# The opening of a selective-scan layer: norms, weights and scratch banks in another order

## The chip, the core and the metric

The kernel runs on one core of a Trainium2 chip. The metric is the time of one execution in microseconds, from the device; lower is better. The engines are named as in the profile: PE (TensorE), PEld (its weight load), DVE (VectorE), ACT (ScalarE), POOL (GpSimd), SP (SyncE, which here only issues DMAs).

## What is computed

Four layers follow one another on an image tensor x of shape (2, 128, 64, 64), all in float32. Only layer 0 is touched here. Cut to what matters, it is:

```
x_norm = layernorm(x over the 128 channels, eps 1e-5) * w + b      # tokens: 4096 per image
for each of 4 token orders (rows, rows reversed, columns, columns reversed):
    xh, z = split(x_norm @ W_in.T)             # 256 inner channels each
    xh    = silu(causal_conv4(xh) + conv_b)
    dt, Bm, Cm = split(xh @ W_xp.T)            # 8, 16, 16 columns
    dt    = softplus(dt @ W_dt.T + b_dt)
    h_t   = exp(dt_t * A) * h_(t-1) + dt_t * Bm_t * xh_t     # 16 states per channel
    y     = (sum_n h_t[n] * Cm_t[n] + xh * Dp) * silu(z)
    out  += (y @ W_out.T) @ W_fuse[order].T
x = x + out + b_fuse
```

Layers 1 and 2 are attention over 4096 tokens, layer 3 is another small scan layer with a group norm.

## The kernel before

Channels lie on the 128 partitions and tokens along the free axis. Layer 0 is cut into 64 chunks of T = 512 tokens: 2 images x 2 orders x forward and reversed x 8. A chunk's 256 channels x 16 states are handled as 16 units of 128 partitions x 1024 elements. For each unit u: POOL forms `dbu` (`s_dbu`, L336), ACT the decay `da` (`s_da`, L349) into one of two PSUM pairs `das`, DVE runs the scan (`s_scan`, L380), DVE or POOL multiplies by C (`s_hc`, L392, L390), and PE sums over states into `y` (`s_y`, L403). Before a chunk's units can run, its front part has to: `px` and `x_` (the convolution folded into four products with `wk`, L238, L243), `xsilu` (L257), `pd` and `xd_` (L273, L278, the columns dt, B and C, whose rows go out to DRAM), `pt`, `abs_`, `e_exp`, `e_ln`, `dt_` (softplus, L293 to L312), `dtu_` (dt times x on POOL, L320), and `spread` and `states` (L328, L287), which store dt, dt times x and the rows of B and C to DRAM and load them back spread over the partitions as `dts`, `dus`, `bs` and `cs`.

The order of the work is written out by hand. Everything inside `tc.manual_schedule()` is issued in program order on each engine, and an engine that waits holds up all that stands behind it in its own order. The declarations above that block (memories set, weights loaded, weights folded) are placed by a planner. The loop over chunks interleaves the front part of the next chunks with the 16 units of the present one through the tables `A`, `V`, `M` and `G`; ahead of this loop stands the opening that is changed.

In the opening, SP loads x in eight pieces of 512 KB (L74). ACT issues the weights' loads: `vec`, `cst`, `m0`, the matrices `mt` (in a buffer of tag `h`), `w_dt` and `cwb` (in one of tag `hc`). DVE forms `wk` from `w_xT` and `cwb` (L125), and PE and DVE fold the output weights into `wof` (L130, L131). A norm of 512 tokens (`Norm0`) is a chain of eleven steps: mean by a product with `meanw` (L167), subtraction (L171), square (L175), variance by products of one column (L180), `keep`, Ln and Exp for the inverse root (L185 to L192), its spread into rows (L197), a product with `ones` (L201), a multiplication (L204) and the affine part into `xn` (L207). Three norms run first, then the front part of chunk 0, its da, dbu and z, the fourth norm, and px, x and silu of chunk 1.

PSUM has eight banks here: `misc` is one, `das` four, `pc` two, `y` one. In the opening every product but `pc` goes into the one bank `misc`:

```
for i in range(2):
    c.px(i)
    c.x_(i)
c.xsilu()
...
norm(3)
for i in range(2):
    c1.px(i)
    c1.x_(i)
c1.xsilu()
c1.pd()
```

Of the kernel before, what the change touches and what calls it, by code (L numbers as in the profile page):

```python
# [7 lines left out]
F32 = mybir.dt.float32  # L8
AF = mybir.ActivationFunctionType
ALU = mybir.AluOpType  # L10
# [3 lines left out]
P = 128  # L14
B, C, H, W = 2, 128, 64, 64
L = H * W
# [35 lines left out]
def _bc(ap, axis, shape):  # L52
    return ap.unsqueeze(axis).to_broadcast(shape)
# [3 lines left out]
def conv_seq_kernel(ctx: ExitStack, tc: tile.TileContext, a: dict, out: bass.AP):  # L57
# [6 lines left out]
    def gt(shape, name, pool=None, **kw):  # L64
        return (pool or gp).tile(shape, F32, tag=name, name=name, **kw)
# [3 lines left out]
    cst = gt([P, _NC], "cst")  # L69
    xin = a["x"].rearrange("b c h w -> c b (h w)")  # L70
    for b in range(B):
        for j in range(4):
            sl = slice(j * L // 4, (j + 1) * L // 4)
            nc.sync.dma_start(x[:, b, sl], xin[:, b, sl])  # L74
    nc.scalar.dma_start(vec, a["vec"])
    nc.scalar.dma_start(cst, a["cst"])
# [1 line left out]
    def v(name):  # L78
        return vec[:, _V[name] : _V[name] + 1]
# [14 lines left out]
    with ExitStack() as c0:  # L94
# [6 lines left out]
        def misc(shape=(P, T)):  # L101
            return ps.tile(list(shape), F32, tag="misc", name="misc")

        def wt(tag, bufs=None, shape=(P, 2, T)):
            return wk_.tile(list(shape), F32, tag=tag, name=tag, bufs=bufs)

        m0 = gt([P, 256 + 2 * ND], "m0", wp)
        nc.scalar.dma_start(m0, a["m0"][:, 0 : 256 + 2 * ND])
        w_zT = m0[:, 0:256]
        w_xpT = m0[:, 256:].rearrange("p (i m) -> p i m", i=2)  # L110

        mt = wt("h", NH, (P, 1024))
        nc.scalar.dma_start(mt, a["m0"][:, 256 + 2 * ND :])
        w_xT, w_out, w_fT = mt[:, 0:256], mt[:, 256:512], mt[:, 512:1024]

        meanw = gt([P, P], "meanw", wp)
        nc.vector.memset(meanw, 1.0 / C)
        w_dt = gt([ND, 256], "w_dt", wp)
        nc.scalar.dma_start(w_dt[64:ND, :], a["wdt"])
        cwb = wt("hc", shape=(P, 4, 256), bufs=NHC)  # L120
        nc.scalar.dma_start(cwb, a["cw0"].partition_broadcast(P))

        wk = gt([P, 4, 256], "wk", wp)
        for k in range(4):
            nc.vector.tensor_mul(wk[:, k, :], w_xT, cwb[:, k, :])  # L125

        wof = gt([P, 2, 4, P], "wof", wp)
        for i in range(2):
            pf = misc()
            mm(pf, lhsT=w_out[:, i * P : (i + 1) * P], rhs=w_fT, start=True, stop=True)  # L130
            nc.vector.tensor_copy(wof[:, i].rearrange("p d c -> p (d c)"), pf)  # L131

        sel = gt([48, NS, 32], "sel", wp)
        nc.vector.tensor_copy(sel[32:48], _bc(cst[32:48, _CI + 32 : _CI + 48], 2, [16, NS, 32]))
        sum4 = cst[:, _CR : _CR + 32]
        diag_d = gt([P, 2, P], "diag_d", wp)
        for i in range(2):
            nc.vector.tensor_scalar(diag_d[:, i, :], ident, v(f"dp{i}"), None, ALU.mult)
        zero = gt([P, 1], "zero", wp)
        nc.vector.memset(zero, 0.0)  # L140
        an = aneg[:, 0:32].rearrange("p (g b) -> p g b", g=4)
# [16 lines left out]
        class Norm0:  # L158
# [6 lines left out]
            def center(self):  # L165
                self.p = misc()
                mm(self.p, lhsT=meanw, rhs=x[:, self.b, self.sl], start=True, stop=True)  # L167
# [9 lines left out]
            def var(self):  # L177
                self.p = misc()
                for k in range(4):
                    mm(self.p[:, k : k + 1], lhsT=self.sq[:, k * P : (k + 1) * P],  # L180
                       rhs=meanw[:, 0:1], start=True, stop=True)
# [12 lines left out]
            def rows(self):  # L194
                self.sq = wt("sq", 1, (P, T))
                for k in range(4):
                    act(self.sq[:, k * P : (k + 1) * P], ident, AF.Copy, scale=self.r[:, k : k + 1])  # L197
# [8 lines left out]
            def affine(self):  # L206
                act(xn[:, self.dst], self.xc, AF.Identity, bias=v("ln_b"), scale=v("ln_w"))  # L207
# [8 lines left out]
        class Chunk:  # L216
# [14 lines left out]
                self.pt_, self.y, self.pc, self.xs = {}, {}, {}, {}  # L231


            def px(self, i):
                self.px_ = misc()
                for k in range(4):
                    off = self.t0 + (6 - k if self.rev else k)
                    mm(self.px_, lhsT=wk[:, k, i * P : (i + 1) * P], rhs=self.src[:, off : off + T],  # L238
                       start=(k == 0), stop=(k == 3))

            def x_(self, i):
                self.xs[i] = wt(f"xs{i}", shape=(P, T))
                act(self.xs[i], self.px_, AF.Identity, bias=v(f"cb{i}"))  # L243

            def pz(self, i):
                self.pz_ = misc()
                mm(self.pz_, lhsT=w_zT[:, i * P : (i + 1) * P],
                   rhs=self.src[:, self.t0 + 3 : self.t0 + 3 + T], start=True, stop=True)

# [16 lines left out]
                self.sz = wt("sz")  # L266
                nc.sync.dma_start(self.sz, gates[self.ci])

            def pd(self):

                self.p = misc()
                for i in range(2):
                    mm(self.p[:ND], lhsT=w_xpT[:, i, :], rhs=self.xs[i],  # L273
                       start=(i == 0), stop=(i == 1))
# [13 lines left out]
                                      self.rows[j, 4 * g + n, :].partition_broadcast(32))  # L288
                (self.cs if j else self.bs)[g] = t

            def pt(self, i):
                self.pt_[i] = misc()
                mm(self.pt_[i], lhsT=w_dt[64:ND, i * P : (i + 1) * P], rhs=self.xd[64:ND, :],  # L293
                   start=True, stop=True)

# [151 lines left out]
            pairs.setdefault(max(m + (3 if m in POOL_HC else 2) for m in (u, u + 1)), []).append(u)  # L447

        with tc.manual_schedule():
            def norm(j):  # L450
                n = Norm0(0, j)
                for f in (n.center, n.sub, n.square, n.var, n.keep, n.ln, n.exp, n.rows, n.scale,
                          n.mul, n.affine):
                    f()

            for j in range(3):
                norm(j)
            c, c1 = chunks[:2]
            for i in range(2):
                c.px(i)  # L460
                c.x_(i)
            c.xsilu()
            c.pd()
            c.xd_()
            for i in range(2):
                c.pt(i)
                c.abs_(i)
            c.e_exp()
            c.e_ln()
            for i in range(2):  # L470
                c.pt(i)
                c.dt_(i)
                c.dtu_(i)
            c.spread("dts", 0)
            c.states(0, 0)
            c.spread("dus", 0)
            for g in range(1, 4):
                c.states(0, g)
            for g in GROUPS_C:
                c.states(1, g)  # L480
            c.spread("dts", 1)
            c.spread("dus", 1)
            for i in range(2):
                c.pz(i)
                c.z_(i)
            c.s_pc(0)
            c.s_dbu(0)
            c.s_dbu(1)
            c.s_da(0)
            c.s_fix(0)  # L490
            norm(3)
            for i in range(2):
                c1.px(i)
                c1.x_(i)
            c1.xsilu()
            c1.pd()
            old = None
            for k, c in enumerate(chunks):
# [485 lines left out]
    with ExitStack() as c3:  # L984
# [65 lines left out]
        class Chunk3:  # L1050
# [17 lines left out]
            def xs_(self):  # L1068
                self.two(flat(lm), lambda i: x[:, self.b, self.sl])
                self.xs = wt("xs", bufs=3)  # L1070
                act(self.xs, self.p, AF.Silu, bias=v("cb3"))
# [418 lines left out]
```

## Time and profile before

| | |
|---|---|
| three timed runs | 6881.41 us median (6864.32 to 6891.15) |
| profiled execution, its own time | 6862.33 us |
| its span | 6860.5 us |
| DVE, POOL, PE, ACT busy over the span | 80%, 78%, 88%, 65% |
| first norm's first product / first px / xd of chunk 0 | 19.92 / 58.84 / 74.11 us |
| scan 0 / scan 1 of chunk 0 | 109.84 / 125.73 us |

Times of single instructions count from the span's start. A row of the time line gives start, duration, engine, line, operation, out<-in with sizes, and in brackets how long the engine had been idle and what released it. Shares over the whole span mix stages with different limits, so the stage that holds the change has to be looked at by itself.

### The profile page before, as it was taken

To read this page: it belongs to the slowest core of one execution; us is meant where nothing else is said; L and a number is where in the kernel's file an instruction comes from. 1 tells how busy PE (TensorE), PEld (TensorE's weight loads), DVE (VectorE), ACT (ScalarE), POOL (GpSimd) and SP (SyncE) were. 2 spreads that over 40 slices of the span, in tenths; PEclk is the share of its full clock that TensorE was granted. 3 is DMA by queue.
4 is the path that set the end of the run, shared out by engine and by line. 5 is a ranking of instruction groups with operands and counts; after the bars stand their busy time and mean duration, and the time that the engine had idled before them with its cause. 6 is when DMAs were issued, how large, how long until landed. Compare 5 with 4: busy or idle time off the path is not lost. (4 is left out here: it accounts for less than half of the span.)

```text
span 6860.5 us, 67328 instructions
## 1 busy us (share of the span) xinstructions
PE 6008.4 (88%) x20656; PEld 2820.0 (41%) x20656; DVE 5521.4 (80%) x4494; ACT 4472.9 (65%) x7688; POOL 5358.9 (78%) x2487
## 2 busy tenths in 40 slices
PE   6888888888888888888879999999999997988888
PEld 1222222222222222222227887787788884222222
DVE  3999999999999999999976665565566665877777
ACT  4887778877788777887756664455456554434343
POOL 3899999899999999999975665555556666777676
PEclk8777777778777777777769999999999998988898
DMA  3555565556565556656640000000000001222222
GB/s 108 139 150 148 148 155 141 138 149 150 142 159 153 150 146 156 155 143 152 155 117 6 3 5 1 1 1 1 1 1 13 1 1 54 69 76 75 87 69 75
DMA packets 352653, 616.52 MB, mean 90 GB/s; under 512 B 72473, under 2 KB 74786, under 8 KB 351906
## 3 DMA queue, kind: packets, MB, share of 16 engines
q1 hardware_dynamic: 351552, 610.44, 34.2%
q8 instruction: 162, 2.65, 0.2%
q14 instruction: 201, 1.65, 0.1%
q10 hardware_dynamic: 738, 1.78, 0.1%
HBM read 496.45 MB, written 115.47 MB: 89 GB/s over the span
## 5 line engine op out<-in xcount | busy, mean ns | idle before, releaser
L336 POOL TENSOR_TENSOR dbu<-dus,bs 128x1024 f32<-128x1024 f32 x1024 | 2402.8, 2372 | 173.0 <-DVE h L380 156.7
L380 DVE TENSOR_TENSOR_SCAN h<-da,hst,dbu 128x1024 f32<-128x1024 f32 x896 | 2090.9, 2341 | 77.3 <-ACT dbu L364 74.6
L349 ACT ACTIVATE da<-dts,aneg 128x512 f32<-128x512 f32 (+1 forms) x2048 | 1411.3, 689 | 438.1 <-DVE h L380 398.2
L832 POOL TENSOR_TENSOR sum<-sum,sc 128x1024 f32<-128x1024 f32 x384 | 906.3, 2360 | 495.6 <-ACT sc L827 491.9
L794 ACT COPY sc<-s 128x512 f32<-128x512 f32 x1024 | 597.9, 585 | 864.6 <-PE s L789 750.5
L789 PE MATMUL s<-q,k 128*128 128x256 f32 x4096 | 1053.3, 380 | 13.3 <-ACT q L775 8.4
L801 DVE TENSOR_TENSOR mx<-mx,s 128x512 f32<-128x512 f32 x896 | 609.4, 680 | 565.5 <-ACT sc L794 564.3
L844 PE MATMUL av<-sc,v 128*128 128x256 f32 x4096 | 1049.7, 379 | 2.3 <-ACT sc L827 2.3
L403 PE MATMUL y<-hc,cst 128*32 128x512 f32 x4096 | 811.6, 759 | 177.9 <-DVE hc L392 103.6
L392 DVE TENSOR_TENSOR hc<-h,pc 128x1024 f32<-128x1024 f32 x704 | 841.2, 1195 | 0.1
L789 PEld LDWEIGHTS s<-q,k 128*128 128x128 f32 x4096 | 777.8, 191 | 146.9 <-issue 36.6
L844 PEld LDWEIGHTS av<-sc,v 128*128 128x128 f32 x4096 | 769.1, 190 | 103.1 <-ACT sc L827 3.7
L390 POOL TENSOR_TENSOR hc<-h,cs 128x1024 f32<-128x1024 f32 x320 | 757.6, 2368 | 1.3 <-issue 1.3
L369 PE MATMUL pc<-xd,sel 16*128 16x512 f32 x1024 | 713.9, 789 | 3.4 <-DVE hc L392 2.6
L1159 POOL TENSOR_TENSOR A<-A,D 128x1024 f32<-128x1024 f32 x224 | 525.5, 2363 | 231.1 <-DVE D L1164 205.0
L824 DVE TENSOR_TENSOR sc<-sc,pm 128x1024 f32<-128x1024 f32 x512 | 620.4, 1212 | 0.9 <-PE pm L820 0.9
L827 ACT ACTIVATE sc<-sc 128x1024 f32<-128x1024 f32 x512 | 541.9, 1059 | 8.6 <-DVE sc L824 8.1
L293 PE MATMUL misc<-xd,w_dt 9*128 9x512 f32 x512 | 394.9, 860 | 157.3 <-ACT x L432 81.6
L1152 ACT ACTIVATE A<-dtr,aneg 128x1024 f32<-128x1024 f32 (+1 forms) x256 | 245.8, 1031 | 382.8 <-PE y L1184 365.3
L403 PEld LDWEIGHTS y<-hc,cst 128*32 128x32 f32 x4096 | 105.7, 117 | 743.2 <-issue 334.8
L1136 PE MATMUL q<-xs,lb 32*128 32x512 f32 x896 | 333.3, 714 | 71.8 <-DVE D L1146 64.8
L1170 DVE TENSOR_TENSOR A<-A,q 128x1024 f32<-128x1024 f32 (+1 forms) x256 | 276.7, 1081 | 141.6 <-PE q L1136 141.2
(210 smaller groups left out, 8079.0 us busy)
## 6 DMA issues: line engine op xcount, KB each, us to landing
dts<-ddt SPq DMA_DIRECT2D x512, 256.0 KB, 5.2
dus<-ddu SPq DMA_DIRECT2D x512, 256.0 KB, 4.8
bs<-rows SPq DMA_DIRECT2D x1024, 64.0 KB, 4.7
cs<-rows SPq DMA_DIRECT2D x1024, 64.0 KB, 3.2
ddt<-dt SPq DMA_DIRECT2D x128, 256.0 KB, 2.0
ddu<-dtu SPq DMA_DIRECT2D x128, 256.0 KB, 2.6
dtr<-ddt SPq DMA_DIRECT2D x448, 64.0 KB, 2.0
rx<-ddx SPq DMA_DIRECT2D x448, 64.0 KB, 1.9
```

The source lines that it names most:

```text
L336: nc.gpsimd.tensor_mul(t, self.dus[q], _bc(self.bs[g], 1, [P, 2, T]))
L349: act(t[:, i, sl], self.dts[q][:, i, sl], AF.Exp, scale=an[:, g, 2 * q + i : 2 * q + i + 1])
L369: mm(t, lhsT=sel[32:48, 4 * g : 4 * g + 4, :].rearrange("p n d -> p (n d)"), rhs=self.xd[32:48, :], start=True, stop=True)
L380: nc.vector.tensor_tensor_scan(ho, ai, bi, init, ALU.mult, ALU.add)
L390: nc.gpsimd.tensor_mul(t, self.h[u], _bc(self.cs[gq(u)[0]], 1, [P, 2, T]))
L392: nc.vector.tensor_mul(t, self.h[u], _bc(self.pc[u // 2], 1, [P, 2, T]))
L403: mm(self.y[q // 2][r : r + 32, :], lhsT=sum4, rhs=self.hc[u][:, i, :], start=False, stop=(u % 8 >= 6), skip_group_check=True)
L789: mm(p[:, o, :], lhsT=j.k[m // 8][:, m % 8 * P : m % 8 * P + P], rhs=self.q, start=True, stop=True)
L801: nc.vector.tensor_max(self.mx, self.s[0][:, 0:2, :] if u == 1 else self.mx, self.p[u])
L824: nc.vector.tensor_sub(s, s, _bc(self.pm[:, :], 1, [P, 4, NQ]))
L832: nc.gpsimd.tensor_add(self.sum, self.s[0] if w == 1 else self.sum, self.s[w])
L844: mm(self.av, lhsT=self.job.v[m // 8][:, m % 8, :], rhs=self.s[u // 2][:, m % 4, :], start=(m == 0), stop=(m == 31))
```

## The change

Only the opening of layer 0 changes, and the helpers that it calls:

- x of each image is loaded in pieces of 1, 1, 2 and 4 chunks in place of four of 2 chunks. The number of loads stays eight.
- ACT's loads are issued in the order `cwb`, `mt`, `m0`, `w_dt`. The folding into `wk`, `wof`, `sel` and `diag_d` moves into the ordered block.
- `px`, `pz`, `pd`, `pt` take a bank as an argument. The opening uses the four banks of `das` (`ba`) and those of `y` and `pc` (`bb`) as scratch.
- The first four norms are written out with their own buffers. The inverse root is Sqrt on ACT and a reciprocal on DVE in place of Ln and Exp. Norm 0 is completed ahead of chunk 0, norm 1 in step with it, norms 2 and 3 in pieces further on.
- `xs_` applies silu straight from the bank of px, in place of an Identity pass and a silu pass.
- On SP the sixteen loads of B precede the store and the spreads of dt. z is copied by DVE. `wof` is formed just ahead of the first scan.

The diff, cut to its core:

```diff
-        for j in range(4):
-            sl = slice(j * L // 4, (j + 1) * L // 4)
+        for lo, hi in ((0, 1), (1, 2), (2, 4), (4, 8)):
+            sl = slice(lo * T, hi * T)
             nc.sync.dma_start(x[:, b, sl], xin[:, b, sl])
...
+        nc.scalar.dma_start(cwb, a["cw0"].partition_broadcast(P))
+        nc.scalar.dma_start(mt, a["m0"][:, 256 + 2 * ND :])
         nc.scalar.dma_start(m0, a["m0"][:, 0 : 256 + 2 * ND])
+        nc.scalar.dma_start(w_dt[64:ND, :], a["wdt"])
...
-            def px(self, i):
-                self.px_ = misc()
+            def px(self, i, p=None):
+                self.px_ = misc() if p is None else p
...
+            def xs_(self, i, p):
+                self.xs[i] = wt(f"xs{i}", shape=(P, T))
+                act(self.xs[i], p, AF.Silu, bias=v(f"cb{i}"))
...
-            for j in range(3):
-                norm(j)
             c, c1 = chunks[:2]
+            ba = [t[:, i, :] for t in das for i in range(2)]
+            bb = [ps.tile([P, T], F32, tag=t, name=t, bufs=n) for t, n in (("y", 1), ("pc", 2), ("pc", 2))]
...
+            def rows(dst, r):
+                for k in range(4):
+                    act(dst[:, k * P : (k + 1) * P], ident, AF.Copy, scale=r[:, k : k + 1])
+            def center(j, xc, p):
+                mm(p, lhsT=meanw, rhs=tokens(j), start=True, stop=True)
+                nc.vector.tensor_sub(xc, tokens(j), p)
+            def scale(xc, sq, p):
+                mm(p, lhsT=ones, rhs=sq, start=True, stop=True)
+                nc.vector.tensor_mul(xc, xc, p)
...
+            center(0, xcs[0], ba[0])
+            act(sqs[0], xcs[0], AF.Square)
+            center(1, xcs[1], bb[0])
+            act(sqs[1], xcs[1], AF.Square)
+            var(ba[1], sqs[0])
+            act(rs[0], ba[1][:, 0:4], AF.Sqrt, bias=eps)
+            nc.vector.reciprocal(rs[0], rs[0])
+            for k in range(4):
+                nc.vector.tensor_mul(wk[:, k, :], w_xT, cwb[:, k, :])
+            rows(sqs[0], rs[0])
+            var(vr, sqs[1])
+            scale(xcs[0], sqs[0], ba[2])
+            affine(0, xcs[0])
+            act(rs[1], vr[:, 0:4], AF.Sqrt, bias=eps)
+            nc.vector.reciprocal(rs[1], rs[1])
+            rows(sqs[1], rs[1])
+            for j in (2, 3):
+                center(j, xcs[j], bb[j - 1])
+            c.px(0, ba[3])
+            c.xs_(0, ba[3])
+            scale(xcs[1], sqs[1], vr)
+            affine(1, xcs[1])
+            c.px(1, ba[0])
+            c.xs_(1, ba[0])
+            c.pd(ba[1])
+            c.xd_()
+            for g in range(4):
+                c.states(0, g)
+            nc.vector.tensor_copy(sel[32:48], _bc(cst[32:48, _CI + 32 : _CI + 48], 2, [16, NS, 32]))
             for i in range(2):
+                nc.vector.tensor_scalar(diag_d[:, i, :], ident, v(f"dp{i}"), None, ALU.mult)
+            for j in (2, 3):
+                act(sqs[j], xcs[j], AF.Square)
             for i in range(2):
+                c.pt(i, ba[2 + i])
                 c.abs_(i)
             c.e_exp()
             c.e_ln()
-            for i in range(2):
-                c.pt(i)
-                c.dt_(i)
-                c.dtu_(i)
+            c.dt_(0)
             c.spread("dts", 0)
+            c.dtu_(0)
             c.spread("dus", 0)
+            c.dt_(1)
+            c.dtu_(1)
             for g in GROUPS_C:
                 c.states(1, g)
             c.spread("dts", 1)
             c.spread("dus", 1)
...
+            for j in (2, 3):
+                var(vr[:, 4 * j : 4 * j + 4], sqs[j])
+            act(r[:, 8:16], vr[:, 8:16], AF.Sqrt, bias=eps)
+            nc.vector.reciprocal(r[:, 8:16], r[:, 8:16])
             for i in range(2):
+                c1.px(i, ba[i])
+            for j in (2, 3):
+                rows(sqs[j], rs[j])
+            for i in range(2):
+                c1.xs_(i, ba[i])
+            c.s_da(0)
             c.s_dbu(0)
             c.s_dbu(1)
-            c.s_da(0)
-            c.s_fix(0)
-            norm(3)
+            c.sz = wt("sz")
             for i in range(2):
+                c.pz(i, bb[1 + i])
+                nc.vector.tensor_copy(c.sz[:, i, :], c.pz_)
+            for j in (2, 3):
+                scale(xcs[j], sqs[j], bb[3 - j])
+                affine(j, xcs[j])
+            for i in range(2):
+                pf = misc()
+                mm(pf, lhsT=w_out[:, i * P : (i + 1) * P], rhs=w_fT, start=True, stop=True)
+                nc.vector.tensor_copy(wof[:, i].rearrange("p d c -> p (d c)"), pf)
+            c.s_pc(0)
             c1.pd()
```

## The prediction

> **What bounds the kernel now.** I read the page's slices first, then the busy time by stretch, then the order of time of the opening, then what each transfer in it took.
>
> ```profile
> DVE  3999999999999999999976665565566665877777
> POOL 3899999899999999999975665555556666777676
> PEclk8777777778777777777769999999999998988898
> ```
>
> One digit is 171.5 us. Layer 0 fills the first 20 to 21 digits with DVE and POOL at 9 or more; the first digit alone reads 3. So the opening is a fill: DVE does nothing that layer 0 is limited by until the scans run. The same by stretch:
>
> ```profile
> 0.00:75.00 75.00, 34.08 (x61) 13.58 (x61) 8.20 (x24) 23.88 (x41) 0.20 (x4) 0.98 0.21 80
> 150.00:3540.00 3390.00, 2877.42 (x7725) 796.10 (x7724) 3246.66 (x1990) 2729.72 (x5202) 3244.21 (x1457) 0.77 0.59 148
> ```
>
> The columns are the stretch, its length, then PE, PEld, DVE, ACT, POOL busy, granted clock, DMA share, GB/s. In the first 75 us DVE is busy for 8.2 us; from 150 to 3540 us it is busy for 3246.7 of 3390, 96%, and POOL as much. The order of the loop over chunks is not touched, so whatever time the steady row of scans starts earlier is time the end comes earlier, if nothing else holds it. Where the fill goes, in order of time:
>
> ```profile
> 19.92 2.08 PE L167 MATMUL misc<-x,meanw 128*128 128x512 f32 x2 [0.78 <-DVE wof L131]
> 22.03 0.69 DVE L171 TENSOR_TENSOR xc<-x,misc 128x512 f32<-128x512 f32 x1 [2.17 <-PE misc L167]
> 22.75 0.63 ACT L175 ACTIVATE sq<-xc 128x512 f32<-128x512 f32 x1 [17.60 <-DVE xc L171]
> 23.44 1.86 PE L180 MATMUL misc<-meanw,sq 128*128 128x1 f32 x8 [1.44 <-ACT sq L175]
> ...
> 25.62 1.28 ACT L189 ACT_TABLE_LOAD   x1
> ...
> 27.14 1.28 ACT L192 ACT_TABLE_LOAD   x1
> ...
> 28.67 1.28 ACT L197 ACTIVATE sq<-cst,r 128x128 f32<-128x128 f32 x4
> 30.00 2.07 PE L201 MATMUL misc<-sq,ones 128*128 128x512 f32 x2 [4.70 <-ACT sq L197]
> 32.11 0.69 DVE L204 TENSOR_TENSOR xc<-xc,misc 128x512 f32<-128x512 f32 x1 [9.39 <-PE misc L201]
> 32.83 0.81 ACT L207 ACTIVATE xn<-xc,vec 128x512 f32<-128x512 f32 x1 [2.89 <-DVE xc L204]
> ...
> 58.84 5.17 PE L238 MATMUL misc<-xn,wk 128*128 128x512 f32 x8 [0.78 <-DVE xc L204]
> ...
> 64.79 3.70 PE L238 MATMUL misc<-xn,wk 128*128 128x512 f32 x8 [0.78 <-ACT xs L243]
> ```
>
> This is one norm as a pure chain: each engine waits for the one before. The next starts at 32.85, so one norm costs 13.0 us, and three stand ahead of the first px at 58.84. The first norm itself starts only at 19.92, behind the folding of the output weights (wof), which waits for the weights' transfers (PE until 11.74, DVE until 14.98) in the single bank misc. The rest of the fill:
>
> ```profile
> 74.11 0.68 ACT L278 ACTIVATE xd<-misc,vec 73x512 f32<-73x512 f32 x1 [2.44 <-PE misc L273]
> ...
> 85.08 0.69 DVE L312 SCALAR_TENSOR_TENSOR dt<-misc,e 128x512 f32<-128x512 f32 x1 [26.30 <-ACT e L306]
> ...
> 102.98 6.94 POOL L336 TENSOR_TENSOR dbu<-dus,bs 128x1024 f32<-128x1024 f32 x3 [12.94 <-DMA bs<-rows]
> ...
> 109.84 2.28 DVE L380 TENSOR_TENSOR_SCAN h<-da,dbu 128x1024 f32<-128x1024 f32 x1
> ...
> 125.73 4.47 DVE L380 TENSOR_TENSOR_SCAN h<-da,dbu 128x1024 f32<-128x1024 f32 x2 [13.61 <-ACT da L349]
> ```
>
> Two things are to be seen: scan 0 stands in DVE's order behind the fourth norm's product (109.23), although its dbu was there at 105.3; and scan 1 waits 13.6 us for ACT, which in its order has the fourth norm, both x of chunk 1 and their silu ahead of the second da. The steady row starts at 125.73. That is the time to beat.
>
> **The change part by part.** I add durations of the rows above. TensorE is costed cold up to the first px (2.08 us for a 128x512 product).
>
> *To the first px.* A 512 KB piece of x took at least 4.0 us from issue (0.74) to landing; a 256 KB piece lands between 3 and 4.8, I take 4.3. Centre 2.08 -> 6.4, sub 0.69 -> 7.1, square 0.63 -> 7.8 (ACT's queue has its last weight DMA out by 6.3). Centre 1 keeps PE until 8.5, var 0 1.86 -> 10.4. ACT squares token chunk 1 until 9.9 and loads the root's table until 11.2; Sqrt 0.26 (layer 3's L1224 takes 0.26) -> 11.5, reciprocal 0.16 (L1228) -> 11.7, rows 1.28 -> 13.0, scale 2.07 -> 15.1. The four wk products stand ahead of DVE's multiply: cwb is now the third transfer on ACT's queue, the matrices the fourth behind 512 KB instead of 201 KB; they landed at 11.7 and I take 13, so wk (1.43) ends at 14.5 and is covered; if they land as late as cwb did before (15.0), 2 us of the next slack are used. Multiply 0.69 -> 15.8, affine 0.81 -> 16.6. But centres 2 and 3 are ahead of px 0 on PE: 15.1 + 4.2 = 19.3. That order costs 2.7 us.
>
> *To xd.* px 0 5.17 -> 24.5; silu straight from PSUM 0.69 (the load was made in ACT's wait) -> 25.2. Scale 1 on PE about 1.2, px 1 3.70 -> 29.4, silu 0.69 -> 30.1, second half of pd 1.2, xd 0.68 -> 32.0. Before: 74.8. Gain 42.8: two norms (26.0), the start at 4.3 instead of 19.9 (15.6), the Identity pass and load of silu (some 3), less PE's order.
>
> *To scan 0.* Squares 2 and 3 (1.26 us ACT) fit in pt 0's wait (2.07). pt 0 -> 34.1, pt 1 in its own bank -> 36.2, abs -> 36.8, Exp and Ln with a load each 2 x 2.34 -> 41.5, dt 0.69 -> 42.2 (10.2 us after xd; before 11.0). On SP the sixteen bs DMAs are now ahead of ddt: rows land about 34.5, 16 x 0.46 us (a row of four took 1.82) end at 41.9, just in time; at the 0.70 each that the twelve beside the spreads took (8.42), ddt would go out 3.5 us late. ddt 0.34 and 2.0 to land -> 44.5, four dts issues -> 46.3, ddu and its landing -> 49, four dus issues -> 50.8, the last 5.7 to land (median of dus in the opening) -> 56.5, dbu 2.35 -> 58.9. Before, dbu 0 began 17.2 us after dt 0; here 14.3, since bs no longer shares the engines with dus.
>
> *To the steady row.* What lies between xd and 58.9 on the other engines: ACT, after Ln at 41.5, has Sqrt with load 1.6, eight rows 2.6, silu load and two silus 2.7, da 0 with load 2.7: 51, or 2 us later if dts lands at 51. PE: vars 3.7, px of chunk 1 3.7 to 7, pz, scales, wof 2.1 each cold: 20 to 24 us from 36.2, so 56 to 60. DVE: two sz copies (0.6 to 0.7 each, off ACT), two multiplies, two wof copies, all behind PE; the last stands directly ahead of scan 0. Its cover is the dus landing; if that cover is gone, wof delays scan 0 by 1 to 2 us. Then POOL gives a dbu every 2.36 us and ACT has no chunk-1 norm left: scan 1 at 61.2. That is 64.5 us before 125.73. The steady row then needs DVE's 3.3 us per scan; POOL needs 10 x 2.36 us for eight dbu, hc 0 and hc 5, less than DVE's 23.7 for scans 1 to 8 (125.73 to 149.43), so the missing stock of three dbu does not bind. What is late next is the dus landing.
>
> *Two rules beside the rows.* Table loads: a load takes 1.28 us in every row and the next activation follows 0.01 us later; each norm pays two, Ln's and Exp's. The Trainium skill, ScalarE: Activation LUTs, sections What ACT_TABLE_LOAD costs and Table sets, says that a switch costs 2.66 us with its drain, and that one set holds exp and ln together while root is another: by it the change trades one load for one, and the switches on the new path (Exp, Ln, with others hidden) would cost 2.8 us more. The trace shows two loads and no drain; I use it: 64.5, by the page 62. Clock: px falls from 0.85 to 0.43 us a pass at 62.1, 3.3 us after it began, and matmuls before it take 1.04 each though the stretch table says clock 1.00 or near, so the durations decide. The skill, TensorE: Matmul & The Clock Gate, Part 1, says that one busy window of about 3.4 us releases the full clock. In the new order PE has nearly no gap from 4 us on, so by the rule centres and px 0 would be at full speed, xd near 28 and the gain 68. The opening before shows no such stretch outside px; I keep it cold.
>
> *Ends for the unknowns.* x piece and weights -1 to +3; PE clock -4 to +2; SP's issue 0 to +3.5; landing of dus -2 to +4. Added up by root of squares about 6 either way: gain 57 to 71.
>
> *Moved at no cost.* The DMAs stay fifteen in the opening and the same on SP after it; sel and diag (0.42 and 2 x 0.29 on DVE) move from the load wait into DVE's wait for dt (26 us before, some 20 now); without that cover they would cost 1.0 us. The two dtu (1.26, POOL) keep their place; dtu 0 is issued behind the dts spread on SP, which is in the sum. Dropping s_fix(0) removes nothing, it returns at once for a first chunk.
>
> The profiled execution took 6862.33 us, 1.83 outside its span. The sum is 6862.3 - 64.5 = 6797.8. That execution is 19.1 under the median 6881.41 of the three timed runs (6864.32 to 6891.15); against the median it is 6817, and I take 6816.
>
> **The rivals.**
> 1. *The spreads are the bound, gain about 45.* If dts and dus take what they took before and SP's issues 0.70 each, and PE stays cold in the waits so that wof ends late, 3.5 + 6 + 4 to 8 us are lost: 6816 + 18 = 6834. For it: dus landed up to 7.9 us after issue. Against: bs was in flight then, and is not now.
> 2. *The start moves, the row does not, under 34.* The first chunk finds no stock of dbu, and chunk 1's chain (pd at the end of PE's list) comes late, so the first chunks refill what was won: it would take 30 us of new stalls, 6848 or more. Against: ACT's 13.6 us wait is gone with its cause.
> 3. *Slower.* One mechanism: TensorE's granted clock in the scan stage. PE is busy for 2877 of 3390 us there at clock 0.77. If another phase of the work gave a lower one, PE would pass DVE's busy time below 0.77 x 2877 / 3247 = 0.68, and to lose the 64.5 us and 34 more the stage must reach 3490 us: 0.77 x 2877 / 3490 = 0.63; time 6915 or more. Against: every 400 us of that stage shows 0.77 to 0.79.
> 4. *Not what it says.* If xn's pieces were ordered against each other as one tile, px 1 would wait for affine 1: 1 us. That decides nothing.
>
> **How the numbers follow.** About 0.5%, 34 us, is what a measurement of this kernel can tell from no change. Forecast 0.70, rival 1 0.17, rival 2 0.08, rival 3 0.05. Faster is the first two less a corner: 0.86. The range takes the forecast's 57 to 71 with the spread of the runs (some 14 us each way) and rival 1: 6788 to 6848.
>
> **What would show it.** Step by step: first centre near 4 us; px 0 near 19; xd near 32; dt 0 near 42; scan 0 near 59, no ACT wait of over 3 us before scan 1, scan 1 near 61; DVE's first digit at 6 instead of 3; DVE and POOL at 96% until some 65 us earlier than 3540; three scan-stage clocks unchanged. It is wrong if scan 0 is early but scan 8 is not near 85 us, if the first DVE wait is for the wof product, or if the stage from 150 us to its end is longer than before.

## The result, and the profile after

The changed kernel takes 6816.7 us (median of 6 runs, 6810.44 to 6822.23), the kernel before 6879.48 us (median of 6, 6860.62 to 6891.15): a ratio of 0.991 (95%: 0.9898 to 0.9921), 62.8 us less. The profiled execution took 6810.44 us with a span of 6808.7, against 6862.33 and 6860.5.

DVE's row of the page after, and busy time by stretch (the stretch, its length, PE, PEld, DVE, ACT, POOL busy, granted clock, DMA share, GB/s):

```profile
DVE  7999999999999999999966665565566675787777
```

```profile
0.00:75.00 75.00, 58.91 (x130) 23.51 (x130) 29.41 (x42) 45.05 (x73) 22.92 (x15) 0.81 0.60 180
95.00:3475.00 3380.00, 2869.62 (x7694) 791.40 (x7692) 3235.88 (x1984) 2723.07 (x5187) 3233.68 (x1452) 0.77 0.60 148
```

One digit is 170.2 us. The first of DVE is 7 where it was 3. In the first 75 us DVE works 29.4 us where it worked 8.2, and PE 58.9 where it worked 34.1. From 95 us on DVE is busy 3235.9 of 3380 us, 96%, at granted clock 0.77: the steady row of scans is what it was, only earlier. The opening in order of time (start, duration, engine, line, operation, count, in brackets the idle time before and what ended it):

```profile
4.01 2.05 PE L460 MATMUL da<-x,meanw 128*128 128x512 f32 x2 [4.01 <-DMA x<-in_x_dram]
...
13.04 2.08 PE L469 MATMUL da<-sq,ones 128*128 128x512 f32 x2 [1.23 <-ACT sq L454]
13.18 1.43 DVE L487 TENSOR_TENSOR wk<-h,hc 128x256 f32<-128x256 f32 x4 [1.51 <-DMA h<-in_m_dram]
14.91 2.69 PE L460 MATMUL pc<-x,meanw 128*128 128x512 f32 x4
17.43 3.60 PE L228 MATMUL da<-xn,wk 128*128 128x512 f32 x8
...
28.07 0.69 ACT L272 ACTIVATE xd<-da,vec 73x512 f32<-73x512 f32 x1 [2.03 <-PE da L267]
...
30.62 2.07 PE L287 MATMUL da<-xd,w_dt 9*128 9x512 f32 x2 [0.69 <-ACT e L294]
...
38.10 1.29 DVE L306 SCALAR_TENSOR_TENSOR dt<-da,e 128x512 f32<-128x512 f32 x2 [14.54 <-ACT e L300]
...
42.69 0.38 SPq L315 DMA_DIRECT2D ddu<-dtu  x1
...
48.08 2.68 SPq L322 DMA_DIRECT2D dus<-ddu  x4
...
54.78 9.24 POOL L330 TENSOR_TENSOR dbu<-dus,bs 128x1024 f32<-128x1024 f32 x4 [13.42 <-DMA ddt<-dt]
57.15 6.89 DVE L374 TENSOR_TENSOR_SCAN h<-da,dbu 128x1024 f32<-128x1024 f32 x3 [4.64 <-POOL dbu L330]
```

Beside the rows of before: the first product starts at 4.01 instead of 19.92, px 0 at 17.43 instead of 58.84, xd at 28.07 instead of 74.11, scan 0 at 57.15 instead of 109.84. The last row is three scans back to back, so scan 1 starts at 59.45 with no wait ahead of it, where it had waited 13.6 us for ACT and started at 125.73. That is 66.3 us earlier. The wait named ahead of dbu (ddt, landed at 40.83) had ended long before; what came last there is dus, whose last piece landed at 54.66.

Where this shift goes later, scan by scan between the two profiled executions: 66.4 us at scan 8, between 63.5 and 69 through the layer, 64.2 at the last of 1024 scans. Some 90 us further on, in the first products of layer 1, it is 58.9; it stays at 58.6 to 58.9 through both attention layers, moves between 55 and 64 in layer 3, and the ends lie 51.8 apart.

### The profile page after: what moved, and what is told of

It reads as the page before. It is cut to its first block, busy times and chain, and to the rows that moved or that the text cites. A ratio compares the mean times of both kernels' runs of the same rounds, so it can differ in the third digit from the quotient of the medians.

```text
span 6808.7 us, 67303 instructions
## 1 busy us (share of the span) xinstructions
PE 6005.6 (88%) x20652; PEld 2821.7 (41%) x20652; DVE 5524.3 (81%) x4499; ACT 4461.8 (66%) x7666; POOL 5362.4 (79%) x2487
## 5 line engine op out<-in xcount | busy, mean ns | idle before, releaser
L847 PE MATMUL s<-q,k 128*128 128x256 f32 x4096 | 1058.0, 382 | 11.7 <-ACT q L833 8.4
L847 PEld LDWEIGHTS s<-q,k 128*128 128x128 f32 x4096 | 781.2, 192 | 146.2 <-issue 36.6
```

The source lines that it names most:

```text
L847: mm(p[:, o, :], lhsT=j.k[m // 8][:, m % 8 * P : m % 8 * P + P], rhs=self.q, start=True, stop=True)
```

## The experiments

In each, "scan 1" is the start of the second scan, since the steady row begins there; the shift is against 125.73 us of the kernel before. The edits to the changed kernel say "after". After itself was profiled twice, with scan 1 at 59.45 and at 58.13 ("after again", the last experiment), so a difference of 1.3 us between two profiles is no effect by itself. Where it matters I count from a common point: dt, the first row of L306, starts at 38.10 in after and 36.71 in after again, and scan 1 follows it by 21.35 and 21.42 us.

### One norm ahead, nothing else (on the kernel before)

```
-            for j in range(3):
-                norm(j)
+            norm(0)
...
             c.spread("dus", 1)
+            for j in (1, 2):
+                norm(j)
```

> The kernel before, with only norm 0 ahead of chunk 0; norms 1 and 2 stand behind the spreads, nothing else moved. Theory one chain (the opening is a single chain through ACT's list and the bank misc, and only its wait for the dts transfer, 97.25 minus 85.05 = 12.2 us, has room): xd moves by 2 x 13.0 = 26 us to 48.8, but the two norms fill that wait and overrun it by 14, so scan 1 comes 12 to 17 us earlier (109 to 114), not 26. Rival what stands ahead of xd counts: scan 1 26 us earlier, near 100. Rival no gain at all because ACT's list is as long: less than 3 us.

6876.76 against 6875.95 us, ratio 1.0001 (0.9992 to 1.0009), scan 1 at 123.57: a shift of 2.2 us. The expected 12 to 17 us did not come. Its opening in order of time:

```profile
48.00 0.68 ACT L278 ACTIVATE xd<-misc,vec 73x512 f32<-73x512 f32 x1 [1.95 <-PE misc L273]
...
62.56 2.08 PE L167 MATMUL misc<-x,meanw 128*128 128x512 f32 x2 [0.78 <-DVE dt L312]
...
74.21 2.07 PE L167 MATMUL misc<-x,meanw 128*128 128x512 f32 x2 [0.78 <-DVE xc L204]
...
87.20 2.08 PE L247 MATMUL misc<-xn,m 128*128 128x512 f32 x2 [0.78 <-DVE xc L204]
...
106.75 2.28 DVE L380 TENSOR_TENSOR_SCAN h<-da,dbu 128x1024 f32<-128x1024 f32 x1
```

xd comes 26.1 us earlier, as two norms of 13 us should give. But norm 1 starts only when the second dt has read `misc` (0.78 us after it), norm 2 when norm 1 has read it, z when norm 2 has. Between 62.56 and 87.20 those two norms cost 24.6 us again, and behind them stand z, the fourth norm and px of chunk 1, all in the same bank. All products but `pc` share that bank, so the opening is nearly a single chain, and this move only shifts two links along it. The wait for dts that I had counted on was no room in the chain: in the kernel before, z and the fourth norm's first product ran through it. Only 1.6 us come back (from that product to its square 2.8 us, not 4.5), and px of chunk 1 takes 6.13 us instead of 5.20: 26.1 - 24.6 + 1.6 - 0.9 = 2.2.

### Only the folded weights late (on the kernel before)

wk's four products go behind norm 0, wof's products and copies go directly ahead of `c1.pd()`.

```
             norm(0)
+            for k in range(4):
+                nc.vector.tensor_mul(wk[:, k, :], w_xT, cwb[:, k, :])
...
+            for i in range(2):
+                pf = misc()
+                mm(pf, lhsT=w_out[:, i * P : (i + 1) * P], rhs=w_fT, start=True, stop=True)
+                nc.vector.tensor_copy(wof[:, i].rearrange("p d c -> p (d c)"), pf)
             c1.pd()
```

> The kernel before, with only the folding of the weights moved: wk behind norm 0, wof ahead of chunk 1's pd; loads of x and weights as before. Theory one chain: norm 0's first product starts at the landing of x's first piece, near 5 us instead of 19.9, wk waits for cwb until 15 and then costs 1.4 beside ACT's work, so xd and scan 1 come 13 to 15 us earlier (scan 1 near 111 to 113), less some 3 us of wof ahead of pd if that reaches scan 1. Rival the weights' transfers are the bound: px cannot start before they land and gains under 5 us.

```profile
4.99 2.05 PE L159 MATMUL misc<-x,meanw 128*128 128x512 f32 x2 [4.99 <-DMA x<-in_x_dram]
...
60.52 0.68 ACT L270 ACTIVATE xd<-misc,vec 73x512 f32<-73x512 f32 x1 [2.06 <-PE misc L265]
...
110.93 6.64 DVE L372 TENSOR_TENSOR_SCAN h<-da,dbu 128x1024 f32<-128x1024 f32 x3
```

6862.83 us, ratio 0.998 (0.997 to 0.9989). The first product starts at 4.99, xd is 13.6 us earlier, scan 1 at 113.12: a shift of 12.6 us, 1.0 less than at xd: scan 0 now stands behind wof's second copy (until 111.0) on DVE, so wof is still paid in part. As expected. No longer waiting for the weights is worth this much by itself.

### After's order in one bank

The norms' products, px, pd and z go to `misc` again (the two pt keep banks of `das`); the order stays after's, with the inverse root of norm 1 ahead of the first scale and chunk 1's px and silu in turns.

```
-            center(0, xcs[0], ba[0])
+            center(0, xcs[0], misc())
...
-            c.px(0, ba[3])
-            c.xs_(0, ba[3])
-            scale(xcs[1], sqs[1], vr)
+            c.px(0)
+            c.xs_(0, c.px_)
+            scale(xcs[1], sqs[1], misc())
```

> The changed kernel with its order kept and the scratch of norms, px, pd and z put back into the single bank misc (only the two pt keep banks of da; the root of norm 1 is taken ahead of the scale of norm 0, since one bank allows no other order). Theory the order carries the gain and the banks are a small part: xd 3 to 5 us later than 28.1, scan 1 3 to 10 us later than 59.4 because z, scales and wof queue up in misc ahead of scan 0. Rival the banks carry it: scan 1 20 us or more later.

```profile
24.02 6.35 PE L228 MATMUL misc<-xn,wk 128*128 128x512 f32 x8 [0.87 <-DVE hc L460]
...
39.51 0.68 ACT L272 ACTIVATE xd<-misc,vec 73x512 f32<-73x512 f32 x1 [2.03 <-PE misc L267]
...
71.99 6.69 DVE L374 TENSOR_TENSOR_SCAN h<-da,dbu 128x1024 f32<-128x1024 f32 x3
```

6827.15 us, ratio 0.9926 (0.9911 to 0.9941). Scan 1 at 74.19, 14.7 us later than after, so 51.5 us of the shift are the order's and 14.7 the banks'. Both theories had this term wrong (3 to 10, and 20 or more). It has two parts. xd is 11.4 us later, of which px 0 itself is 2.75: its eight products take 6.35 us here and 3.60 in after, since PE pauses for each reader of the bank and px starts slow. The remaining 3.3 come behind xd, where z and chunk 1's products queue again.

Together with the first experiment this shows what the order is worth: 2.2 us when only norms 1 and 2 are moved, 51.5 when everything else of the change but the banks comes with them (the weights, the pieces of x, the root, the pieces of all the norms, silu, pt, the rows of B, z), though nearly all of it is still in one bank.

### Ln and Exp instead of Sqrt and reciprocal (after)

```
-            act(rs[0], ba[1][:, 0:4], AF.Sqrt, bias=eps)
-            nc.vector.reciprocal(rs[0], rs[0])
+            act(rs[0], ba[1][:, 0:4], AF.Ln, bias=eps)
+            act(rs[0], rs[0], AF.Exp, scale=-0.5)
```

The same for the other two roots.

> The changed kernel with Ln and Exp(-0.5) in place of Sqrt and reciprocal in the first four norms. By the trace each pair costs two loads of 1.28 us: first px and xd 1 to 3 us later (norm 0's root 1.3 longer, less what px waits for PE; norm 1's in PE's time), scan 1 within 3 us. By the rule that one table set holds both, xd would be the same or earlier. The number of loads before scan 0 tells it apart.

```profile
9.44 1.28 ACT L484 ACT_TABLE_LOAD   x1
11.02 1.28 ACT L485 ACT_TABLE_LOAD   x1
...
17.54 1.28 ACT L492 ACT_TABLE_LOAD   x1
19.12 1.28 ACT L493 ACT_TABLE_LOAD   x1
...
58.81 6.89 DVE L374 TENSOR_TENSOR_SCAN h<-da,dbu 128x1024 f32<-128x1024 f32 x3 [5.67 <-POOL dbu L330]
```

Scan 1 at 61.11, 1.7 us later than after and 3.0 later than after again; xd, counted from the first product of each run, 1.8 and 2.4 us later. That is the direction and size of the trace's count. One time, 6810.17 us, tells nothing at this size. Ln and Exp pay a load each, 1.28 us apiece, in both norms; with the root there is one load for norm 0 (9.90 in after) and none for norm 1. The rule of one table set for both, which the prediction weighed, does not show here. So the root saves something, and little.

### All norms ahead of the first px (after)

Squares, variances, root, rows, scale and affine of norms 2 and 3 go directly ahead of `c.px(0, ba[3])`.

> The changed kernel with norms 2 and 3 completed ahead of chunk 0's first px, in their own banks and buffers; nothing else moved. After the one-norm run, where moving norms behind xd alone won 2 us, the question is whether the place of the norms is worth anything once the banks are apart. Theory it is: the pieces are 1.1 of squares, 3.6 of variances, 0.7 root, 2.5 rows, 2.1 scales on the path, so px, xd and scan 1 come 8 to 10 us later. Rival the gain is in banks and in the early start alone: scan 1 under 3 us later, because PE and ACT had room.

```profile
26.39 4.37 PE L228 MATMUL da<-xn,wk 128*128 128x512 f32 x8
...
37.80 0.68 ACT L272 ACTIVATE xd<-da,vec 73x512 f32<-73x512 f32 x1 [2.03 <-PE da L267]
...
66.49 6.89 DVE L374 TENSOR_TENSOR_SCAN h<-da,dbu 128x1024 f32<-128x1024 f32 x3 [11.05 <-POOL dbu L330]
```

Scan 1 at 68.79, 9.3 us later than after, within the expected 8 to 10 (10.7 later than after again; 8.6 and 10.0 counted from the first product); one time of 6815.27 us. With banks of their own, two norms side by side cost 9.3 us ahead of the chain, not the 26 of two norms in a single bank.

### The rows of B behind the spreads, as before (after)

```
-            for g in range(4):
-                c.states(0, g)
...
             c.spread("dts", 0)
+            c.states(0, 0)
...
             c.spread("dus", 0)
+            for g in range(1, 4):
+                c.states(0, g)
```

> The changed kernel with the loads of B back where they were: four behind the dts spread, twelve behind the dus spread. SP was through with the sixteen at 37.7, before dt was there (38.8), so nothing is won ahead of ddt; ddu and dus are issued 2 us later and share the engines with bs: scan 0 and scan 1 2 to 5 us later. Rival the order on SP is without effect: under 1 us either way.

```profile
58.44 6.89 DVE L374 TENSOR_TENSOR_SCAN h<-da,dbu 128x1024 f32<-128x1024 f32 x3 [5.40 <-POOL dbu L330]
```

ddu is issued at 44.36 instead of 42.69, dus at 49.02, and scan 1 starts at 60.74: 1.3 us later than after, which is no more than two profiles of after differ. Counted from dt (37.91) it is 1.5 later, less than the expected 2 to 5, in the direction expected. 6816.28 us, one time.

### dt times x stored ahead of dts (after)

```
+            c.dtu_(0)
             c.spread("dts", 0)
-            c.dtu_(0)
```

> The changed kernel with dt times x of channels 0 to 127 formed and stored ahead of the dts spread, so that ddu is issued near 40.2 in place of 42.7 and does not have to land beside a megabyte of dts (5.4 us). Theory the landing of dus is what scan 0 waits for: dus is issued from 42.7 in place of 48.1, shares the engines with dts, and scan 0 comes 3 to 4 us earlier (53 to 54.5), scan 1 at 55.5 to 57. Rival DVE's wof copy (to 52.5) or da is right behind: less than 1 us.

```profile
39.02 0.34 SPq L315 DMA_DIRECT2D ddu<-dtu  x1
39.71 1.78 SPq L322 DMA_DIRECT2D dts<-ddt  x4
41.59 1.80 SPq L322 DMA_DIRECT2D dus<-ddu  x4
...
51.18 9.24 POOL L330 TENSOR_TENSOR dbu<-dus,bs 128x1024 f32<-128x1024 f32 x4 [10.95 <-DMA ddt<-dt]
...
53.56 6.88 DVE L374 TENSOR_TENSOR_SCAN h<-da,dbu 128x1024 f32<-128x1024 f32 x3 [4.27 <-POOL dbu L330]
```

dus goes out at 41.59 instead of 48.08, with no wait, and scan 1 is 3.6 us earlier than after's (55.85), in the expected range. But 1.1 of that was there before the edit acts: dt starts at 36.96 instead of 38.10, since pt's second product took 1.12 us in this execution and 2.07 in after's. Counted from dt, dus is issued 5.4 us earlier, dbu and scan 1 come 2.5 us earlier: the right direction, but less than the 3 to 4 expected. 6807.29 us, one time. The transfers from issue to landing, of after and then of this kernel (line, engine, count, KB each, median us to landing, from 35 to 60 us):

```profile
ddu<-dtu SPq DMA_DIRECT2D x2, 256.0 KB, 5.4
```

```profile
ddu<-dtu SPq DMA_DIRECT2D x2, 256.0 KB, 2.0
dus<-ddu SPq DMA_DIRECT2D x8, 256.0 KB, 7.6
```

The store takes 5.4 us behind the 1 MB of dts and 2.0 ahead of it; the dus loads, now beside dts, take 7.6 us. In after they took 4.1.

### Banks that are truly apart for pd and pt (after)

```
-            c.pd(ba[1])
+            c.pd(bb[0])
...
-                c.pt(i, ba[2 + i])
+                c.pt(i, (ba[2], bb[1])[i])
```

> The changed kernel with pd and the second pt in banks outside the pair that the step before uses. In the trace pd's first half waited for the silu of x 1 and pt 1 for the first abs, though each had a bank to itself: theory, the two banks of one da tile are ordered as one. Then pd starts at px 1's end (25.3 in place of 26.1), pt 1 follows pt 0 without a wait, dt 0 comes 1.5 to 2.5 us earlier and scan 1 as much. Rival: the wait is for data, and nothing moves.

```profile
25.46 2.02 PE L267 MATMUL y<-xs,m 128*73 128x512 f32 x4
25.66 0.69 ACT L233 ACTIVATE xs<-da,vec 128x512 f32<-128x512 f32 x1 [1.90 <-PE da L228]
...
29.22 1.02 PE L287 MATMUL pc<-xd,w_dt 9*128 9x512 f32 x2
...
29.88 7.26 SPq L281 DMA_DIRECT2D bs<-rows  x16
...
35.64 0.69 DVE L306 SCALAR_TENSOR_TENSOR dt<-da,e 128x512 f32<-128x512 f32 x1 [11.78 <-ACT e L300]
...
37.23 0.37 SPq L308 DMA_DIRECT2D ddt<-dt  x1
```

pd starts before the second silu, and the second product of pt follows the first with no wait, where after waits 0.69 us for abs ahead of it (its row at 30.62). So the two halves of one `da` tile were ordered as one by the program. dt is 2.5 us earlier than in after; 1.8 of it are the edit's (0.9 from px 1 to xd and 0.9 from xd to dt, against after again), the rest is mostly the speed of pt's second product again. But ddt cannot go out at 36.3: SP is still issuing the sixteen bs, from 29.88 for 7.26 us. Scan 1 at 58.63 is 0.8 us earlier than in after and 0.5 later than in after again, so no gain is shown, where 1.5 to 2.5 were expected; 6811.02 us, one time. Against after again, whose first product started 0.6 us sooner, the 1.8 won by dt are nearly all lost again: some 1.1 between dt and the issue of dts, most of it SP's sixteen issues, and 0.5 in the transfers behind.

### All of it, and after again beside it

The two edits before this, with squares of norms 2 and 3 ahead of px 1, the scale and affine of norm 1 behind xd's work, and eight of the sixteen bs behind the first dus:

```
-            scale(xcs[1], sqs[1], vr)
-            affine(1, xcs[1])
+            for j in (2, 3):
+                act(sqs[j], xcs[j], AF.Square)
...
-            for g in range(4):
+            for g in range(2):
                 c.states(0, g)
+            scale(xcs[1], sqs[1], vr)
+            affine(1, xcs[1])
...
             c.spread("dus", 0)
+            for g in range(2, 4):
+                c.states(0, g)
```

> The changed kernel with the findings of the runs before put together: pd and the second pt in banks apart, squares 2 and 3 in ACT's wait for px 1, norm 1's scale and affine behind xd, eight of the sixteen loads of B ahead of ddt and eight behind the dus spread (with the banks apart SP's sixteen became what ddt waited for: 37.23 against dt at 36.3), ddu ahead of the dts spread. If the dus landing stays what scan 0 waits for: xd at 26 to 27.5, dt 0 near 33.5, scan 1 at 51 to 54, 5.5 to 8.5 us earlier than the changed kernel, and some 6 us, 0.1%, off the time. Rival: wof on DVE, or the loads of B behind dus, hold scans 0 to 4: under 3 us and nothing in the time.

> The changed kernel itself, for the comparison in the same runs: 0.991 of the time before, scan 1 at 59.4 within 1 us (the opening does not depend on the run).

```profile
26.65 0.68 ACT L272 ACTIVATE xd<-y,vec 73x512 f32<-73x512 f32 x1 [1.17 <-PE y L267]
...
49.31 9.24 POOL L330 TENSOR_TENSOR dbu<-dus,bs 128x1024 f32<-128x1024 f32 x4 [11.27 <-DMA bs<-rows]
...
51.69 6.89 DVE L374 TENSOR_TENSOR_SCAN h<-da,dbu 128x1024 f32<-128x1024 f32 x3 [2.91 <-ACT xd L272]
```

And of after again:

```profile
30.18 1.12 PE L287 MATMUL da<-xd,w_dt 9*128 9x512 f32 x2 [0.69 <-ACT e L294]
...
55.83 6.89 DVE L374 TENSOR_TENSOR_SCAN h<-da,dbu 128x1024 f32<-128x1024 f32 x3 [6.79 <-POOL dbu L330]
```

Scan 1 starts at 53.98, 5.5 us before after's 59.45 and 4.1 before the 58.13 of after in the same set of runs: at the edge of what was expected, or below it. Scan 0 waits for dbu, and dbu for the last piece of dus, which landed at 49.19. The last scan starts 72.7 us earlier than before's, where after again is 64.9 there. In the time the 6 us are not to be seen: 6794.1 us, ratio 0.9884 (0.9869 to 0.9899), beside 6791.06 us, ratio 0.988 (0.9863 to 0.9896), for after, 4 runs each.

After again missed its own expectation, 59.4 within 1 us. The difference begins with PE: the second product of pt took 1.12 us here and 2.07 in the first profile, and dt came 1.4 us sooner. And after's ratio is 0.991 in one set of runs and 0.988 in the other, with intervals that do not meet: a gain of 62.8 us in the one and 83.2 in the other (6874.3 before).

## Why the prediction was right, point by point

6816 us was forecast and 6816.7 came, 62.8 below the median of before where the sum had 64.5. Faster, as forecast, and none of the rivals. The mechanism held: the row of scans starts 66.3 us earlier, runs as before, and hands on most of that. That the number was met to a microsecond is in part luck: PE's clock was costed too slow and ddu too fast, in opposite directions, and the second set of runs shows a gain of 83.2. The steps:

**To the first px.** Forecast 4.3 for the first product, 19.3 for px 0; measured 4.01 and 17.43. The order that puts centres 2 and 3 ahead of px 0 cost what was said in kind, but less: those two took 2.69 us together, not 4.2.

**The clock of PE: the step that failed.** I costed PE cold (at the slow passes of the opening before) up to the first px, and weighed the Trainium skill's rule (TensorE: Matmul & The Clock Gate, Part 1: one busy window of about 3.4 us releases the full clock) against it. For px 0 and xd the rule came nearer. The products at 13.04 still take 1.04 us a pass; those from 14.91 on take 0.67 in the mean, with weight loads 0.85 us apart at first and 0.43 apart from 16.6 on, 3.5 us after 13.04 without a gap between products; and px 0 takes 3.60 us, 0.45 a pass, where I had 5.17. The one-bank experiment is the other half of the evidence: the same order with pauses gives px 0 at 6.35 us, with weight loads 0.85 us apart for the first 5 us. xd came at 28.07, the rule's "near 28", not 31.3, with its end at 28.76 where 32.0 was forecast. As I had applied the rule, with full speed from the first centre on, it failed: the first two centres took over 1 us a pass, and although PE was busy for 7.4 of the 9 us from 4 to 13, the products at 13.04 were slow. Pauses are not the whole account either: with no pause from the first product on, the first eight variance products took 0.95 us in the run with the rows of B behind and 1.81 in the run with Ln and Exp. What sets the moment was not found.

**To dt.** 10.2 us after xd were forecast, 10.0 measured (28.76 to 38.79). The near hit is luck: pt 0 ran at 1.12 us instead of 2.07, and that paid for pt 1's wait of 0.69 us, which the ordering of the pair brought and the sum had left out. In after again, with both pt fast, it is 9.1. One more thing neither the list of changes nor the sum has: the kernel before forms pt twice, since `misc` is overwritten (L293 at 74.85, 77.61, 80.36 and 85.83), and there dts goes out at 90.48, 5.4 us after dt; after forms it once, and dts goes out 2.7 us after dt (40.84).

**SP.** The sixteen bs ended at 37.69, ahead of dt at 38.8: "just in time" held, and the experiment with banks apart shows that it holds only just: with dt 0 through at 36.3, ddt goes out 0.9 us later than it could.

**To scan 0.** Forecast 16.7 us from dt to scan 0, measured 18.4. The mis-sized term is ddu: issue and landing together were put at 2.7 us, and its store, issued at 42.69 behind four dts loads of 256 KB each, landed at 48.06, 5.4 us later. SP stood still for it:

```profile
SPq L322 <- DMA ddu<-dtu: 4.9, 1, 4.9
```

(This is after's list of waits between 30 and 60 us: total, times, longest.) Storing ddu ahead of dts brings the landing back to 2.0 and, counted from dt, scan 0 forward by 2.5. The dus landing was overestimated in the other direction, 5.7 for 3.9 (50.75 to 54.66), and its four issues took 2.7, not 1.8. The two dtu products and wof were covered as said: wof's last copy ended at 52.5, and DVE then waited 4.64 us for dbu. "Late next is the dus landing" was right.

**To the steady row.** Scan 1 came behind scan 0 with no wait for ACT, 59.45 for 61.2; scan 8 at 83.0 for "near 85". So no stall is handed on, and the want of a stock of dbu is not felt (rival 2). Rival 1 would have needed 79 for scan 1. Rival 3 needed a clock of 0.63; it is 0.77, and DVE's share is 96% in both. Rival 4 is not seen: px 1 starts at 21.72, ahead of the affine part of norm 1 (22.65).

Its parts can be told from the experiments: 12.6 us for the weights' folding behind the norm, 14.7 for the banks, 9.3 for norms 2 and 3 behind the first px; some 2 for the root instead of Ln and Exp and some 1.5 for the bs ahead, these two from single profiles and little above what profiles of one kernel differ by. They are not to be added, as each is taken out of another kernel; the first and the 51.5 of the order in one bank say how much of it needs the order as a whole. (One count in the prediction is wrong and changes nothing: the opening has fourteen loads, eight of x and six of ACT's, not fifteen.)

**What stays open.** In the profiled pair 64.2 us at the last scan become 58.9 in the first products of layer 1 and 51.8 at the end. No line of layers 1 to 3 is changed. The traces show where it goes: PE runs slower there in after's execution. At the start of layer 1 (L789 before, L847 after) ten passes behind the first gap take 0.43 us each where they take 0.22 in before. At the end of layer 3 each step's four products take twice as long; a row of before and one of after:

```profile
6825.47 1.13 PE L1136 MATMUL q<-xs,lc 32*128 32x512 f32 x4
```

```profile
6773.60 2.08 PE L1194 MATMUL q<-xs,lc 32*128 32x512 f32 x4
```

The last five steps take 19.0 us where they take 9.9. It does not follow the kernel: after again, the same program, has the slow start of layer 1 too (64.9 become 59.5), but the fast end of layer 3, and ends 66.5 us earlier than before; the kernel with only the folded weights late has the slow start, the one-bank kernel the fast one. From the last scan to the end the profiled executions take 3317 to 3341 us (before 3324, after 3337, after again 3323). So I take the loss for PE's speed in those layers and not for an effect of the change. What sets that speed was not found, and neither was what makes the medians gain 62.8 us in one set of runs and 83.2 in the other.

## What to carry to other kernels

In a fill ahead of a saturated row, first ask what orders the fill: where nearly every step writes into one scratch bank, moving one step can do no more than move its place in the same chain (2.2 us from 26). Reordering the whole fill still paid in one bank (51.5 us), and banks that are idle until the row begins added 14.7 here. Put ahead only what the first unit of the row needs, and count the transfers of the fill in the order of their queue: a store that a later load depends on goes ahead of large loads that nobody needs yet (2.5 us). Each gain has a next cover; the one after dt was SP's sixteen issues, to be read off the trace before the edit. And profile the same kernel twice before reading a gain of a microsecond or two off one trace.

## What the runs showed that was not expected

A store behind large loads on the same queue was late: the 256 KB of ddu took 5.4 us behind 1 MB of dts, 2.0 ahead of it. In the kernel with ddu ahead, the transfers themselves seem to become the bound. The stretch table of after and of that kernel, from the spread's beginning to dbu (the column before the last is the DMA share):

```profile
41.00:48.00 7.00, 6.98 (x18) 2.83 (x17) 1.38 (x2) 4.48 (x10) 0.36 (x1) 1.00 0.78 187
48.00:55.00 7.00, 5.92 (x13) 1.65 (x11) 2.76 (x4) 5.42 (x9) 0.22 (x1) 1.00 0.79 223
```

```profile
41.00:51.00 10.00, 9.20 (x21) 3.08 (x19) 4.14 (x6) 7.32 (x12) 0.00 (x0) 1.00 1.04 241
```

The DMA engines are busy for 78% of the time in after and for all of it with ddu first, where they move 241 GB/s. That fits why, counted from dt, 5.4 us at the issue became 2.5 at dbu: a better order of these transfers has little left to give. It was not tested with fewer bytes or larger pieces, and 241 GB/s is what these transfers reach, not what the engines can move: loading x and the weights (4 to 13 us of after) they move 391 at a share of 1.01.

PE's speed in one place differs between two executions of one kernel: 2.07 and 1.12 us for the second product of pt, 2.08 and 1.13 for the four products at the end of layer 3. And the profile's granted clock does not show whether PE is slow in an opening: it reads 1.00 from 20 to 45 us of before, where a 512-column pass takes 1.04 us, and from 17.4 to 25.3 us of after, where it takes 0.45. There the duration of a pass is the evidence.
